# One edge tile in ten groups fetched row by row on the SyncE queue

## The chip, the cores and the metric

One core of one Trainium2 chip. Times are device microseconds (us) of that core; a run's time is its whole execution, and the time before is the median of three runs.

## The reference

One message-passing layer of a graph network, after a layer norm, with a residual. There are 12,500 nodes with 64 features and 412,500 edges with 32 features, sorted by their receiver. Cut to what matters:

```python
h = maximum(layernorm(x), 0)
msg_in = concat([h[senders], h[receivers], edge_features])      # 64 + 64 + 32
messages = silu(msg_in @ W1 + b1) @ W2 + b2                     # 64 wide
att = softmax(silu(msg_in @ Wa1 + ba1) @ Wa2 + ba2, axis=0)     # over all edges
aggregated = segment_sum(messages * att, receivers)
return x + silu(concat([h, aggregated]) @ Wu1 + bu1) @ Wu2 + bu2
```

## The kernel before

**First stage (to about 100 us).** For every node the sender's and the receiver's share of the first layer, both attention and message half, 128 numbers, are computed once and stored in the tables `ts_d` (senders) and `tr_d` (receivers) in device memory. A row of either is 512 bytes.

**The loop over groups.** Edges go in tiles of 128 and in groups of K = 8 tiles; there are NG = 403 groups. `one_pass` runs over them in a software pipeline written out by hand: at step g it calls `begin(g)`, then `load(g + 2)`, then `end(g)`, with pieces of the sums of earlier groups (`sum_up`) between.

- `load(g)` asks for everything of group g. On POOL, eight indirect DMAs (line 382), one per tile, each fetch 128 rows of `ts_d` by the edges' sender numbers, which lie in `src_sb`; they fill the eight planes of the tile `gs`, of which there are eight buffers. On SP, every four groups (NQ = 4), one DMA brings the edge features (`eo`, line 391), two bring the receivers' numbers (`db`, line 394), and one register load (line 369, called by `registers`) brings the first receiver of four groups at once. For each group two more SP DMAs (line 401) fetch a window of rows of `tr_d` into `wins`, at an address from such a register; there are three window buffers. DVE then makes a one-hot matrix in `eo` (line 405), and PE multiplies it, with the edge features below it, by the window (line 409), into the PSUM tile `pe`: the receiver's and the edge's share.
- `begin(g)` adds the gathered sender's share: DVE `gs = pe + gs` (line 414), then ACT takes the tanh (line 415).
- `end(g)` forms messages and attention logits on DVE. Every fourth group a running maximum is taken; later steps weigh the messages and sum them by receiver through PE (lines 477 to 508).

**Work beside the loop.** Between groups 16 and about 116, `node_bias` and `node_rest` (lines 276 to 305) prepare the update of the nodes; their loads and stores go through SP as well (lines 285, 294, 303, 305).

**Last stage (from about 4108 us).** The update of all nodes.

**Order.** Compute instructions of the loop stand in the order in which the program is written (`pin`). DMAs and register loads are not pinned: a scheduler puts them into their engine's stream by program order and by what it takes to be ready. [...]

Of the kernel before, what the change touches and what calls it, by code (L numbers as in the profile page):

```python
# [42 lines left out]
F32 = mybir.dt.float32  # L43
I32 = mybir.dt.int32
AF = mybir.ActivationFunctionType
ALU = mybir.AluOpType
AX = mybir.AxisListType
ENG = mybir.EngineType
# [3 lines left out]
P = 128  # L52
# [3 lines left out]
C = 2 * U  # L56
S1 = U + 1
K = 8
# [7 lines left out]
B = 4  # L66
NQ = 4
TABLES = 4
EPS = 1e-5
NEG = -3.0e38  # L70
BIG = 3.0e38
# [5 lines left out]
WHY = "a receiver's number; windows past the last node are padded"  # L77


@with_exitstack  # L80
def gnn_kernel(ctx: ExitStack, tc: tile.TileContext, n_edges, x, src, dst, dst_row, first, edge,
               weights, out):
    nc = tc.nc
    NB = x.shape[0] // P
    T = src.shape[1]
    NG = T // K
    NP = NB * P
# [6 lines left out]
    ts_d = dram.tile([NP, C], F32, name="ts_d")  # L94
# [12 lines left out]
    part, at = {}, 0  # L107
# [45 lines left out]
    with tc.tile_pool(name="node1", bufs=1) as node1, \  # L153
# [20 lines left out]
        pin = tc.keep_in_program_order  # L174
# [15 lines left out]
        eps = node1.tile([P, 1], F32, name="eps")  # L190
        nc.vector.memset(eps, EPS)
        xms, sqs, rstds, hs = {}, {}, {}, {}
# [60 lines left out]
        for c, nn in chunks:  # L253
            tr = node.tile([P, CB, C], F32, name="tr")[:, :nn, :]
            for b in range(0, nn, 4):
                n = min(4, nn - b)
                pn = node_ps.tile([P, 4, C], F32, name="pn", bufs=4)
                for i in range(0, n, 2):
# [8 lines left out]
        windows()  # L267

    one_pass(tc, n_edges, locals())
    again = nc.values_load(wrong[0:1, 0:1], min_val=0, max_val=1,  # L270
                           skip_runtime_bounds_check_because="it is the outcome of a comparison")
# [36 lines left out]
def one_pass(tc, n_edges, v):  # L308
    nc = tc.nc
    NB, T, NG, NP, CB = (v[k] for k in ("NB", "T", "NG", "NP", "CB"))  # L310
# [3 lines left out]
    ts_d, tr_d, bq_d, edge, dst_row = (v[k] for k in ("ts_d", "tr_d", "bq_d", "edge", "dst_row"))  # L314
# [8 lines left out]
    pin = tc.keep_in_program_order  # L323

    with ExitStack() as ctx:
# [16 lines left out]
        for w in wins:  # L342
            nc.vector.memset(w, 0.0)
            for r in range(2):
                rows = slice(WR + r * DE, WR + (r + 1) * DE)
                nc.vector.tensor_copy(w[rows, :, r, :], we[rows, None, :].to_broadcast([DE, 2, C]))
        with tc.tile_pool(name="work2", bufs=2) as work2, \
                tc.tile_pool(name="small", bufs=3) as small, \
                tc.tile_pool(name="pre_ps", bufs=AHEAD + 1, space=PSUM) as pre_ps, \
                tc.tile_pool(name="one_ps", bufs=1, space=PSUM) as one_ps:  # L350
            pes, gss, lgs, ps_, psums, sps, pps, ees, mts = ({} for _ in range(9))


            w2t_ps = one_ps.tile([P, 4, P], F32, name="mt")[:U, 0, :S1]
# [4 lines left out]
            nc.tensor.matmul(w2u_ps, w2t, wu1a, start=True, stop=True)  # L359
            nc.vector.tensor_copy(w2u, w2u_ps)  # L360
            at_sp, at_dve = {}, {}


            tr_w = bass.AP(tensor=tr_d.tensor, offset=tr_d.offset,
# [2 lines left out]
            def registers(g, engine, at):  # L367
                n = min(NQ, NG - g)
                _, regs = nc.values_load_multi_w_load_instructions(
                    base_sb[0:1, g:g + n], engines=[engine], min_val=0, max_val=NP - 1,  # L370
                    skip_runtime_bounds_check_because=WHY)
                for i in range(n):
                    at[g + i] = regs[i]

            def load(g):

                t = g * K
                if g % NQ == 0:
                    registers(g, ENG.SP, at_sp)
                gs = gss[g] = gather.tile([P, K, C], F32, name="gs")  # L380
                for j in range(K):
                    nc.gpsimd.indirect_dma_start(  # L382
                        out=gs[:, j, :], out_offset=None, in_=ts_d[:, :],
                        in_offset=bass.IndirectOffsetOnAxis(ap=src_sb[:, t + j:t + j + 1], axis=0))
                if g % NQ == 0:
                    n = min(NQ, NG - g) * E2
                    eo = work2.tile([P, NQ, E2], F32, name="eo")
                    db = work2.tile([WR, NQ, E2], I32, name="db")
                    for i in range(g, min(g + NQ, NG)):
                        ees[i] = eo[:, i - g, :], db[:, i - g, :]  # L390
                    nc.sync.dma_start(eo.rearrange("p g e -> p (g e)")[WR:, :n],
                                      edge[:, g * E2:g * E2 + n])
                    for r in range(2):
                        nc.sync.dma_start(
                            db.rearrange("p g e -> p (g e)")[r * R:(r + 1) * R, :n],
                            bass.AP(tensor=dst_row.tensor, offset=dst_row[r:r + 1, g * E2:].offset,
                                    ap=[[0, R], [1, n]]))
                eo, db = ees.pop(g)
                win = wins[g % WINS]
                for r in range(2):  # L400
                    nc.sync.dma_start(win[r * R:(r + 1) * R, :, r, :],
                                      tr_w[bass.ds(at_sp[g], R), :, :])
                for h in range(2):
                    e = slice(h * E2 // 2, (h + 1) * E2 // 2)
                    pin(nc.vector.tensor_scalar(eo[:WR, e], db[:, e], bj[:, g, h:h + 1], None,  # L405
                                                op0=ALU.is_equal))
                pe = pes[g] = pre_ps.tile([P, K, C], F32, name="pe")
                for q in range(H):
                    pin(nc.tensor.matmul(pe[:, 2 * q:2 * q + 2, :], eo[:, q * P:(q + 1) * P],  # L409
                                         win[:, q // 2, :, :], start=True, stop=True))  # L410

            def begin(g):

                pin(nc.vector.tensor_tensor(gss[g], pes[g], gss[g], ALU.add))  # L414
                pin(nc.scalar.activation(pes[g], gss[g], AF.Tanh))  # L415

            def end(g):
# [94 lines left out]
            at, weighed = [None, None], [0]  # L512
# [28 lines left out]
            for g in range(AHEAD):  # L541
                load(g)
            done = 0
            for g in range(NG):
# [3 lines left out]
                if more and g == NG - 1:  # L548
                    next(more)
                begin(g)  # L550
                if more and g < NG - 1:
                    next(more)
# [6 lines left out]
                if g + AHEAD < NG:  # L559
                    load(g + AHEAD)  # L560
# [36 lines left out]
        with tc.tile_pool(name="upd1", bufs=1) as upd1, \  # L597
# [14 lines left out]
            for c in range(0, NB, 2 * H):  # L612
                n = min(H, (NB - c) // 2)
# [32 lines left out]
def general(tc, n_edges, v, dst):  # L646
# [7 lines left out]
    with ExitStack() as ctx:  # L654
        keep = ctx.enter_context(tc.tile_pool(name="keep_g", bufs=1))
        act_d = dram.tile([P, T, S1], F32, name="act_d")
        sum_d = [dram.tile([NP + P, S1], F32, name=f"sum_d{r}") for r in range(TABLES)]
        before = keep.tile([P, P], F32, name="before")
# [15 lines left out]
        rows = (NP + P) // P  # L674
        for r in range(TABLES):
            flat = sum_d[r].rearrange("(p b) f -> p (b f)", p=P)
# [63 lines left out]
        with tc.tile_pool(name="sums_g", bufs=2) as work, \  # L740
                tc.tile_pool(name="sums_g_ps", bufs=2, space=PSUM) as sums_ps:
            for g in range(0, T, G):
# [3 lines left out]
                for k in range(0, ng, K):  # L746
# [26 lines left out]
                    for j in range(K):  # L773
                        nc.gpsimd.indirect_dma_start(
                            out=sum_d[(t + j) % TABLES][:, :],
                            out_offset=bass.IndirectOffsetOnAxis(ap=to[:, j:j + 1], axis=0),
# [6 lines left out]
        with tc.tile_pool(name="upd_g", bufs=2) as work, \  # L783
                tc.tile_pool(name="upd_g_ps", bufs=2, space=PSUM) as upd_ps:
            for c in range(0, NB, CB):
                part = work.tile([P, TABLES, CB, S1], F32, name="part")
                for r in range(TABLES):
                    nc.sync.dma_start(part[:, r], sum_v[r][:, c:c + CB, :])
                for r in range(1, TABLES):
                    nc.vector.tensor_tensor(part[:, 0], part[:, 0], part[:, r], ALU.add)  # L790
# [95 lines left out]
```

## Time and profile before

| | |
|---|---|
| median of three runs | 4173.35 us (4166.1 to 4174.21) |
| profiled execution: its own time | 4166.68 us |
| its span, first to last instruction | 4164.9 us |
| busy: POOL, DVE, PE, ACT | 73%, 69%, 54%, 14% |
| mean share of the 16 DMA engines | about 35% |
| granted TensorE clock | 0.635 |

The page lists groups of instructions by line, with busy time, mean duration and the idle time of the engine just ahead of them. SP runs no computation; what it does is issue DMAs and load registers, so it has no busy time on the page, and its queue is read from the views by source line and from its own waits ("SPq"). The shares are averages over three stages. The loop, from about 105 to 4100 us, is 96% of the span.

### The profile page before, as it was taken

The numbers are of one execution on the slowest core, as the hardware profiler recorded it, in microseconds if no ns is written. First come the engines' busy times: TensorE is split into PE (matmuls) and PEld (weight loads), VectorE is DVE, ScalarE is ACT, GpSimd is POOL, SyncE is SP. The second block draws the span as 40 slices with busy tenths as digits, with TensorE's granted clock in tenths as the row PEclk, the third lists the DMA queues.
The fourth block names the chain that finished last, engine by engine and source line by source line (L and its number), as shares of the span: only waits on it lengthen the run. The fifth ranks groups of instructions, "written<-read, shape, count | busy, mean of one in ns | idle before, by whom it ended". The sixth has DMA issues, their size and how long they took to land.

```text
span 4164.9 us, 43769 instructions
## 1 busy us (share of the span) xinstructions
PE 2237.8 (54%) x10980; PEld 1678.3 (40%) x10980; DVE 2873.2 (69%) x7698; ACT 600.9 (14%) x1230; POOL 3052.8 (73%) x3236
## 2 busy tenths in 40 slices
PE   5544555545545555555555455555555555555555
PEld 4433434333434343443444334343344443444444
DVE  5867767766677676666766667666676666666668
ACT  2211111111111111111111111111111111111112
POOL 3777777777777777777777777777777777777772
PEclk8666666666666666666656655666565666656665
DMA  7433433333333333333333332333323333333323
GB/s 269 103 92 95 102 100 96 101 95 101 101 89 90 89 81 90 82 88 90 80 90 83 87 89 80 90 82 87 90 80 89 83 88 90 80 90 85 85 77 111
DMA packets 230871, 392.46 MB, mean 94 GB/s; under 512 B 97745, under 2 KB 156370, under 8 KB 217426
## 3 DMA queue, kind: packets, MB, share of 16 engines
q0 software_dynamic: 103168, 211.49, 19.1%
q1 hardware_dynamic: 125778, 167.76, 15.2%
q10 hardware_dynamic: 1664, 10.32, 0.6%
q8 instruction: 91, 1.49, 0.1%
q14 instruction: 170, 1.39, 0.1%
HBM read 363.56 MB, written 25.72 MB: 93 GB/s over the span
## 4 chain that ended last, share of the span: by engine, by line


## 5 line engine op out<-in xcount | busy, mean ns | idle before, releaser
L382 POOL DMA_INDIRECT gs<-ts_d,src_sb x3224 | 3051.2, 946 | 1038.3 <-issue 930.2
L409 PE MATMUL pe<-wins,eo 128*128 128x256 f32 x3224 | 1395.8, 608 | 1178.2 <-issue 1122.1
L409 PEld LDWEIGHTS pe<-wins,eo 128*128 128x128 f32 x3224 | 953.6, 310 | 1453.1 <-issue 1189.0
L414 DVE TENSOR_TENSOR gs<-pe,gs 128x1024 f32<-128x1024 f32 x403 | 491.8, 1220 | 1116.6 <-DMA gs<-ts_d,src_sb 1103.8
L415 ACT ACTIVATE pe<-gs 128x1024 f32<-128x1024 f32 x403 | 415.7, 1031 | 2760.5 <-DVE gs L414 2267.5
L477 DVE TENSOR_SCALAR wt<-iota_w,dloc,p 128x40 f32<-128x40 f32 x3224 | 725.2, 316 | 0.1
L483 PE MATMUL sp<-wt,acts 128*65 128x40 f32 x6448 | 586.0, 261 | 0.9 <-DVE wt L477 0.9
L483 PEld LDWEIGHTS sp<-wt,acts 128*65 128x65 f32 x6448 | 535.3, 173 | 26.7 <-DVE wt L477 1.0
L453 PE MATMUL mt<-ident,mx 128*128 128x128 f32 x103 | 48.6, 472 | 530.3 <-DVE sums L507 526.9
L425 DVE SCALAR_TENSOR_TENSOR acts<-pe,gs 128x512 f32<-128x512 f32 x403 | 271.9, 675 | 27.7 <-ACT pe L415 27.6
L433 DVE TENSOR_TENSOR pe<-pe,w_all 128x512 f32<-128x512 f32 x403 | 281.4, 698 | 12.8
L431 DVE SCALAR_TENSOR_TENSOR pe<-pe,gs 128x512 f32<-128x512 f32 x403 | 280.4, 696 | 11.2
L436 DVE TENSOR_REDUCE lg<-pe 128x8 f32<-128x512 f32 x403 | 276.9, 687 | 10.3
L405 DVE TENSOR_SCALAR eo<-db,bj 64x256 f32<-64x256 int32 x806 | 270.3, 373 | 8.0 <-DMA db<-in_dst_row_dram 0.4
L494 PEld LDWEIGHTS mt<-ss,w2u 65*64 65x64 f32 x806 | 99.2, 175 | 392.6 <-issue 378.6
L453 PEld LDWEIGHTS mt<-ident,mx 128*128 128x128 f32 x103 | 18.8, 182 | 543.1 <-DVE sums L507 538.9
L494 PE MATMUL mt<-ss,w2u 65*64 65x40 f32 x806 | 149.9, 280 | 160.5 <-DVE gm L460 148.0
L464 ACT ACTIVATE scale<-fall 128x1 f32<-128x1 f32 x103 | 20.9, 203 | 510.2 <-DVE fall L463 510.2
L508 DVE COPY sums<-nmax 64x40 f32 x403 | 79.1, 196 | 9.0 <-issue 0.2
L489 ACT COPY ss<-sp 65x40 f32<-65x40 f32 x403 | 73.5, 182 | 28.6 <-PE sp L483 28.6
L507 DVE TENSOR_TENSOR sums<-sums,mt 64x40 f32 x300 | 53.6, 179 | 3.5 <-PE mt L494 2.4
L290 ACT COPY bu<-mt 64x512 f32<-64x512 f32 x24 | 25.9, 1078 | 149.1 <-PE mt L287 149.1
(89 smaller groups left out, 591.3 us busy)
## 6 DMA issues: line engine op xcount, KB each, us to landing
gs<-ts_d,src_sb POOLq DMA_INDIRECT x3224
eo<-in_edge_dram SPq DMA_DIRECT2D x100, 512.0 KB
db<-in_dst_row_dram SPq DMA_DIRECT2D x200, 256.0 KB
wins<-tr_d SPq DMA_DIRECT2D x806, 32.0 KB
ts_d<-ts SPq DMA_DIRECT2D x5, 896.0 KB
tr_d<-tr ACTq DMA_DIRECT2D x5, 896.0 KB
hT_d<-hT ACTq DMA_DIRECT2D x1, 3136.0 KB
hb<-in_x_dram SPq DMA_DIRECT2D x24, 128.0 KB
```

What stands on the lines that cost most here:

```text
L382: nc.gpsimd.indirect_dma_start(out=gs[:, j, :], out_offset=None, in_=ts_d[:, :], in_offset=bass.IndirectOffsetOnAxis(ap=src_sb[:, t + j:t ...
L405: pin(nc.vector.tensor_scalar(eo[:WR, e], db[:, e], bj[:, g, h:h + 1], None, op0=ALU.is_equal))
L409: pin(nc.tensor.matmul(pe[:, 2 * q:2 * q + 2, :], eo[:, q * P:(q + 1) * P], win[:, q // 2, :, :], start=True, stop=True))
L414: pin(nc.vector.tensor_tensor(gss[g], pes[g], gss[g], ALU.add))
L415: pin(nc.scalar.activation(pes[g], gss[g], AF.Tanh))
L425: pin(nc.vector.scalar_tensor_tensor(acts[g % ACTS][:, :, 0:U], th[:, :, U:C], 1.0, gs[:, :, U:C], op0=ALU.add, op1=ALU.mult))
L431: pin(nc.vector.scalar_tensor_tensor(att, th[:, :, 0:U], 1.0, gs[:, :, 0:U], op0=ALU.add, op1=ALU.mult))
L433: pin(nc.vector.tensor_tensor(att, att, wa2[:, None, :].to_broadcast([P, K, U]), ALU.mult))
L436: pin(nc.vector.tensor_reduce(lgs[s][:, k:k + K], att, AX.X, ALU.add))
L477: pin(nc.vector.tensor_scalar(wt[:, j, :], iota_w[:, j // H, :], dloc[:, g * K + j:g * K + j + 1], p[:, k + j:k + j + 1], op0=ALU.is_equal ...
L483: pin(nc.tensor.matmul(sp, acts[g % ACTS][:, j, :], wt[:, j, :], start=j == 0, stop=j == K - 1))
L494: pin(nc.tensor.matmul(pp, w2u, sps.pop(g), start=True, stop=True))
```

## The change

In 39 of the 403 groups (g = 10, 20, ... 390) the last of the eight tiles is no longer gathered by POOL. Its 128 rows are fetched by 128 DMAs from SP, one row and one partition each, into a tile of its own, `one_gs`.

- The sender numbers of the tile come as one row of a new input, `src_row`, which holds the same numbers as `src` in their order; `rows_ahead` asks for them five groups before the first row is fetched.
- `rows(g)`, called in `load(g)` just after the windows, fetches ROWS = 13 rows (11 in the last of ten groups) of the tile that is due ten groups later. Register loads bring the row numbers, LOADS = 4 at a time: four loads in a group of 13 rows, for 4, 4, 4 and 1 numbers.
- `begin(g)` adds seven planes of `gs` in one instruction and the eighth, from `one_gs`, in another.

The last tile asked for is that of group 390, as 400 is not below NG - 4 = 399.

```diff
--- before.py
+++ after.py
@@ -66,6 +66,9 @@
 B = 4
 NQ = 4
 TABLES = 4
+EVERY = 10
+ROWS = 13
+LOADS = 4
 EPS = 1e-5
 NEG = -3.0e38
 BIG = 3.0e38
@@ -78,7 +81,7 @@
 
 
 @with_exitstack
-def gnn_kernel(ctx: ExitStack, tc: tile.TileContext, n_edges, x, src, dst, dst_row, first, edge,
+def gnn_kernel(ctx: ExitStack, tc: tile.TileContext, n_edges, x, src, src_row, dst, dst_row, first, edge,
                weights, out):
     nc = tc.nc
     NB = x.shape[0] // P
@@ -348,7 +351,7 @@
                 tc.tile_pool(name="small", bufs=3) as small, \
                 tc.tile_pool(name="pre_ps", bufs=AHEAD + 1, space=PSUM) as pre_ps, \
                 tc.tile_pool(name="one_ps", bufs=1, space=PSUM) as one_ps:
-            pes, gss, lgs, ps_, psums, sps, pps, ees, mts = ({} for _ in range(9))
+            pes, gss, lgs, ps_, psums, sps, pps, ees, mts, alone = ({} for _ in range(10))
 
 
             w2t_ps = one_ps.tile([P, 4, P], F32, name="mt")[:U, 0, :S1]
@@ -360,6 +363,35 @@
             nc.vector.tensor_copy(w2u, w2u_ps)
             at_sp, at_dve = {}, {}
 
+            rows_at, rows_to = {}, {}
+
+            def rows_ahead(g):
+                if g < NG - 4:
+                    t = g * K + K - 1
+                    rows_at[g] = small.tile([1, P], I32, name="one_src", bufs=2)
+                    nc.sync.dma_start(rows_at[g], v["src_row"][:, t * P:(t + 1) * P])
+
+            def rows(g):
+                if g == 0:
+                    rows_ahead(EVERY)
+                if g % EVERY == 0:
+                    rows_at.pop(g, None)
+                    rows_to.clear()
+                    if g + EVERY in rows_at:
+                        rows_to[g + EVERY] = one = work2.tile([P, C], F32, name="one_gs")
+                        alone[g + EVERY] = one
+                if g % EVERY == EVERY // 2:
+                    rows_ahead(g + EVERY // 2 + EVERY)
+                for at, to in rows_to.items():
+                    i = g % EVERY * ROWS
+                    for a in range(i, min(i + ROWS, P), LOADS):
+                        n = min(LOADS, P - a)
+                        _, regs = nc.values_load_multi_w_load_instructions(
+                            rows_at[at][0:1, a:a + n], engines=[ENG.SP], min_val=0, max_val=NP - 1,
+                            skip_runtime_bounds_check_because=WHY)
+                        for k in range(n):
+                            nc.sync.dma_start(to[a + k:a + k + 1, :], ts_d[bass.ds(regs[k], 1), :])
+
 
             tr_w = bass.AP(tensor=tr_d.tensor, offset=tr_d.offset,
                            ap=[[C, NP + WR - SHIFT], [SHIFT * C, 2], [1, C]])
@@ -378,7 +410,7 @@
                 if g % NQ == 0:
                     registers(g, ENG.SP, at_sp)
                 gs = gss[g] = gather.tile([P, K, C], F32, name="gs")
-                for j in range(K):
+                for j in range(K - (g in alone)):
                     nc.gpsimd.indirect_dma_start(
                         out=gs[:, j, :], out_offset=None, in_=ts_d[:, :],
                         in_offset=bass.IndirectOffsetOnAxis(ap=src_sb[:, t + j:t + j + 1], axis=0))
@@ -400,6 +432,7 @@
                 for r in range(2):
                     nc.sync.dma_start(win[r * R:(r + 1) * R, :, r, :],
                                       tr_w[bass.ds(at_sp[g], R), :, :])
+                rows(g)
                 for h in range(2):
                     e = slice(h * E2 // 2, (h + 1) * E2 // 2)
                     pin(nc.vector.tensor_scalar(eo[:WR, e], db[:, e], bj[:, g, h:h + 1], None,
@@ -411,7 +444,10 @@
 
             def begin(g):
 
-                pin(nc.vector.tensor_tensor(gss[g], pes[g], gss[g], ALU.add))
+                n = K - (g in alone)
+                pin(nc.vector.tensor_tensor(gss[g][:, :n, :], pes[g][:, :n, :], gss[g][:, :n, :], ALU.add))
+                if n < K:
+                    pin(nc.vector.tensor_tensor(gss[g][:, n, :], pes[g][:, n, :], alone.pop(g), ALU.add))
                 pin(nc.scalar.activation(pes[g], gss[g], AF.Tanh))
 
             def end(g):
@@ -863,6 +899,7 @@
     arrays = {
         "x": padded(x, nb * P),
         "src": np.ascontiguousarray(padded(src, t * P).reshape(t, P).T),
+        "src_row": padded(src, t * P)[None],
         "dst": np.ascontiguousarray(dst_row.reshape(t, P).T),
 
         "dst_row": np.ascontiguousarray(dst_row.reshape(t // 2, 2, P).transpose(1, 0, 2).reshape(2, -1)),
```

## The prediction

> **What bounds the kernel now.** The page's busy table comes first, then its costliest groups. The page's chain that ended last is empty for this run, so the bound has to be read from groups and waits.
>
> ```profile
> PE 2237.8 (54%) x10980; PEld 1678.3 (40%) x10980; DVE 2873.2 (69%) x7698; ACT 600.9 (14%) x1230; POOL 3052.8 (73%) x3236
> L382 POOL DMA_INDIRECT gs<-ts_d,src_sb x3224 | 3051.2, 946 | 1038.3 <-issue 930.2
> ```
>
> POOL is at 73%, DVE at 69%; neither looks full. But POOL's idle time in front of the gathers is 930 us of "issue": it waits for nobody, it needs that time itself. The timeline of POOL shows the beat:
>
> ```profile
> 2011.29 0.94 POOL L382 DMA_INDIRECT gs<-ts_d,src_sb  x1 [0.30 <-issue]
> 2012.54 0.94 POOL L382 DMA_INDIRECT gs<-ts_d,src_sb  x1 [0.30 <-issue]
> 2013.79 0.94 POOL L382 DMA_INDIRECT gs<-ts_d,src_sb  x1 [0.30 <-issue]
> ```
>
> 0.94 busy and 0.30 between: one gather each 1.25 us, eight a group, 10.0 us a group. The first starts at 56.4 and the last at 4091.0 (the view of line L382), so (4091.0 - 56.4) / 3223 = 1.252 us is the beat of the whole loop, start to end. POOL bounds the kernel. The waits, longest first, agree: DVE's longest own wait is for what POOL fetched, and POOL's wait for others is small.
>
> ```profile
> DVE gs L414 <- DMA gs<-ts_d,src_sb: 1103.8, 274, 14.6
> ...
> POOL gs L382 <- DMA gs<-ts_d,src_sb: 60.8, 193, 1.7
> ```
>
> **SP, where the new work goes.** Its queue is in the waits of SP and in the views by source line (min/median/max ns):
>
> ```profile
> SPq L401 <- PE pe L409: 1877.9, 264, 22.2
> ...
> SPq L305 <- DVE hb L304: 117.2, 25, 7.8
> SPq L616 <- PE mt L494: 57.0, 1, 57.0
> SPq L303 <- PE mt L287: 45.9, 23, 3.3
> ...
> SPq L285 <- DMA xb_d<-hb: 37.2, 24, 1.9
> ```
>
> ```profile
> L401 SPq DMA_DIRECT2D wins<-tr_d x806: 316/317/938, 92.1 to 4050.8; - x162
> ```
>
> ```profile
> L369 SPq TENSOR_LOAD <-base_sb x101: 294/299/1443, 86.0 to 4022.7; - x101
> ```
>
> ```profile
> L166 SPq DMA_DIRECT2D base_sb<-in_first_dram x1: 307/307/307, 7.0 to 7.0; - x1
> ```
>
> SP is ahead: it mostly waits for PE to give back one of three windows (L401). The lines L303, L305 and L285 are the node work, which lies between 109 and 1168 us only (first and last start); their waits are for results just asked for, so they are not all slack.
>
> **What the Trainium skill says.** "DMA: Bandwidth & Descriptors", section "Issuing engines are not separate DMA queues": issuing from another engine saves only sequencer time. Here that time is just what binds (1.25 us of POOL a gather), so moving a gather can pay. Same page, "Why a DMA increments its semaphore by 16 and not by 1": a DMA from SP whose slowest dimension gives one engine is put on that one, and the sequencer itself writes the rest of the semaphore. The one single-partition DMA of this trace, base_sb, took SP 0.307 us, no more than the others. Same page, "Latency and other measured facts": about 600 ns for a register load; this trace has 0.299 us for four registers, and I use that.
>
> **The change, part by part.** Groups 10, 20, ... 390 qualify (400 is past NG - 4 = 399): 39 tiles.
>
> Removed: 39 gathers, 39 x 1.252 = **48.8 us** of POOL. Ten groups then take it 79 x 1.252 = 98.9 us, not 100.2.
>
> Added on SP per tile: 128 row DMAs, 9 x 4 + 3 = 39 loads, one ask for row numbers. A window DMA with a register in its address: a pair spans 0.82 to 0.84 us in the timeline and one is 0.317, so the next starts 0.51 later; 0.19 of it is address arithmetic and turn-round. With 0.307 for one partition: 0.50 a row. From below 0.44 (arithmetic partly shared), from above 0.62 (a separate wait in front, or an issue as slow as hT_d's 0.606). 128 x 0.50 = 64.0. Loads: 0.30 and 0.05 to the next, 39 x 0.35 = 13.7; from above, at the skill's 0.6, 25, as most of these loads do not start at a multiple of four numbers. The ask: 0.4. Sum **78.1 us per ten groups**.
>
> SP's present work, without waits, per four groups: 8 x 0.51 windows, eo 0.53, db 0.43 + 0.63, load 0.35, six waits' handling 0.3: 6.3, so 15.7 per ten groups. Node work adds per four groups 0.45 + 0.44 + 2 x 0.65 + 0.54 + 0.2 = 2.9, so 7.4 per ten.
>
> So SP needs 93.8 of POOL's 98.9 us in the late stage, but **101.2 of 98.9 in the node stage** (groups 16 to 116), before any wait. SP is in order; the trace shows eight completion semaphores in turn on its queue, each DMA waiting for the one eight before. A row lands, I estimate, like a window (median 1.7 us in the records) and eight rows take 4; only eo (5.1 us to land) makes SP wait, an estimated 0.6 per four groups, 1.5 per ten. The node work's waits (117.2 + 45.9 + 37.2 + 16.6 for L294) / 25 = 8.7 us per four groups; rows stand in them now, and I keep a third, 2.9, which is 7.2 per ten: from below 0, from above all, 22. Node stage: 101.2 + 1.5 + 7.2 = 109.9.
>
> What is queued behind: the windows, which PE needs (L409), then DVE's L414. How much lateness is free? Windows can start at 92.1; PE at about 94 + 9.5 g if SP paces, the gathers land at 68 + 9.9 g (56.4, one group's 9.9, some 2 to land). So at group 16 the loop is 20 us behind POOL, where now it has caught up (DVE takes 6.4 us a group at 126 to 145 us). POOL stops when gather g + 8 finds none of the eight buffers free: at 56.4 + 79 + 9.9 g, so 135 + 9.9 g; with some 10 us from the matmul to the end of a group, lateness of 55 us is free. Node stage: 10 x (109.9 - 98.9) = 110 more, 130 in all, 75 beyond the cover. Net 75 - 48.8 = **26 us slower**. Later SP has about 3.5 us to spare per ten groups and regains the rest before the end; the last 13 groups have no rows.
>
> DVE: L414 split in two, one more instruction and up to eight semaphore waits, some 0.2 + 0.4 us in 39 groups, 23 us in all, covered by DVE's 31% idle time; if DVE were the bound, they would count. The rows' bytes replace the gather's, so DMA load (33%) stays.
>
> The profiled execution took 4166.7 us (span 4164.9, 1.8 around it): 4193. The median of the runs, 4173.35, lies 6.7 above it: **4199**.
>
> **Rivals.**
> 1. SP keeps up. For: 93.8 in the late stage, and the node waits may vanish as rows fill them. Then up to 102.4 us per ten groups in the node stage are free, and the whole 48.8 comes: 4125. The point of no change is 107.3. Chance of a visible gain 0.28.
> 2. The forecast, SP late in the node stage alone: 4182 to 4260. With it, near no change: 0.09; slower 0.40.
> 3. SP bounds the whole loop, for instance with 0.56 to a row because each needs a wait of its own (0.055): 103 late (4.1 over, 28 times), 117.6 in the node stage: 115 + 187 + 20 - 55 - 49 = 218 slower: 4391. The point is 98.9 / 128: a row price of 0.53. Chance 0.19.
> 4. The rows run in bursts: DMAs without a fixed place can be ordered ahead (db goes out before older windows at 2006 to 2010 us). 128 rows in front of a window are 78 us, against three windows and 55 us of cover; some 25 us a tile, 39 times: 5100. Chance 0.04.
> That the gathers are not dropped (3224 stays) would leave 4173 plus SP's work; the code shows no reason.
>
> **How the numbers follow.** A measurement of this kernel can tell about 0.2% (8 us). Faster 0.28 (rival 1), within 0.09, slower 0.40 + 0.19 + 0.04 = 0.63. Predicted is the likeliest case, 4199; its own range is 4182 to 4260. The range for 8 in 10 reaches from rival 1 (4122) into rival 3 (4350): 0.12 lie above, a little below.
>
> **What would show it.** Gathers 3185; row DMAs 4992 at about 0.31 us on SP; SP's wait for PE at L401, 1878 us, down below 400; in the node stage POOL with gaps over 0.3 us, waiting for DVE, and PE waiting for wins; after 1200 us POOL at its 1.25 beat. Wrong if POOL never waits (rival 1), or if PE's waits for wins run to the end (rival 3).

## The result and the profile after

The changed kernel takes 5286.07 us (median of 4 runs, 5277.05 to 5286.85) against 4173.66 us before: ratio 1.266, interval 1.265 to 1.268. That is 1112 us slower; the forecast was 26 us slower, with a range that ended at 4350.

The page after, its busy line and its costliest groups:

```profile
PE 2333.5 (44%) x10980; PEld 1741.0 (33%) x10980; DVE 2884.4 (55%) x7737; ACT 615.0 (12%) x1230; POOL 3015.5 (57%) x3197
...
L414 POOL DMA_INDIRECT gs<-ts_d,src_sb x3185 | 3014.0, 946 | 2171.0 <-issue 2090.1
L442 PE MATMUL pe<-wins,eo 128*128 128x256 f32 x3224 | 1484.6, 640 | 2734.0 <-DMA wins<-tr_d 1131.3
...
L438 DVE TENSOR_SCALAR eo<-db,bj 64x256 f32<-64x256 int32 x806 | 252.2, 351 | 1213.1 <-DMA db<-in_dst_row_dram 1106.8
```

The 39 gathers are gone (3185) and each of the others costs what it did (946 ns). But POOL's idle time has grown from 1038 to 2171 us, PE waits 1131 us for windows and DVE 1107 us for receivers' numbers. Both come through SP. That POOL's "issue" is now a wait shows in the view of the gathers' line, where an EVENT_SEMAPHORE is POOL's queue waiting for a free buffer; the first line is before, the second after:

```profile
L382 POOLq EVENT_SEMAPHORE  x399: 17/43/43, 52.9 to 4074.7; - x200
```

```profile
L414 POOLq EVENT_SEMAPHORE  x399: 17/3492/20662, 52.9 to 5169.9; - x200
```

Before, such an instruction takes 43 ns, so the buffer is free; after, the median is 3.5 us and the longest 20.7. POOL has become a follower. SP's own waits, where before the wait for PE at the windows' line stood at 1877.9 us, now read:

```profile
SPq L393 <- DMA db<-in_dst_row_dram: 56.7, 109, 1.2
...
SPq L433 <- PE pe L442: 20.8, 4, 7.4
```

SP no longer waits for PE: it is the bound. What fills it is in the views of its new lines (min/median/max ns):

```profile
L393 SPq DMA_DIRECT2D one_gs<-ts_d x6045: 224/228/292, 95.8 to 5107.8; - x195
L393 SPq EVENT_SEMAPHORE  x682: 17/17/17, 107.1 to 5102.2; - x171
```

```profile
L389 SPq TENSOR_LOAD <-one_src x1521: 301/1117/1731, 95.2 to 5105.9; - x191
```

Two things here are not as forecast. The row DMAs are 6045, not 4992: 155 a tile instead of the 128 that the description of the change has too. And a register load takes 1.117 us in the median, not 0.30. Issuing a row is cheaper than assumed, 0.228 us instead of 0.307.

**Why 155.** The loop over a group runs from i to i + 13 in steps of four, and `n = min(LOADS, P - a)` looks only at the end of the tile. The load at i + 12 so brings four numbers and fetches rows i + 12 to i + 15, and the next group fetches the last three again: 9 x 16 + 11 = 155. The description's loads of "4, 4, 4 and 1 numbers" are 4, 4, 4 and 4. A second fetch of a row has to wait for the first, with an EVENT_SEMAPHORE in front: the view has 682, and the kernel with sixteen rows a group below, which fetches no row twice, has none on that line. They cost little, some 0.08 us each in the records.

**Why 1.1 us.** A group's numbers begin at a multiple of 13. The view of the load line in two windows of time, first in a group that begins at row 52, then in the next, at row 65:

```profile
L389 SPq TENSOR_LOAD <-one_src x4: 310/554/597, 2534.6 to 2542.6; - x4
```

```profile
L389 SPq TENSOR_LOAD <-one_src x5: 1062/1124/1145, 2546.4 to 2559.1; - x5
```

Over all tiles the records give one pattern (medians): where the first number is a multiple of four (16 bytes) the load takes 0.55 us behind a row and 0.31 or 0.48 behind a window's DMA; elsewhere it takes 1.12 behind a row and 0.87 or 1.06 behind a window's DMA. The lower of each pair stands in every fourth group, where SP has loaded the windows' registers just before. The last load of a tile, of three numbers off a multiple, takes 0.93. Behind DMAs of the node work loads take longer still, up to 1.73. Three groups of ten (rows 0, 52, 104) begin on a multiple of four.

**The order of SP's stream.** The timeline of SP after shows the windows each between sixteen rows, as the program has them, and in the whole trace no more than 16 rows stand between two groups' windows, so nothing ran ahead in bursts:

```profile
2505.81 0.86 SPq L433 DMA_DIRECT2D wins<-tr_d  x2
2508.04 10.54 SPq L393 DMA_DIRECT2D one_gs<-ts_d  x16
2518.83 0.86 SPq L433 DMA_DIRECT2D wins<-tr_d  x2
2521.05 10.20 SPq L393 DMA_DIRECT2D one_gs<-ts_d  x16
2531.35 0.48 SPq L423 DMA_DIRECT2D eo<-in_edge_dram  x1
2531.89 1.04 SPq L426 DMA_DIRECT2D db<-in_dst_row_dram  x2
2533.73 0.87 SPq L433 DMA_DIRECT2D wins<-tr_d  x2
2535.14 9.73 SPq L393 DMA_DIRECT2D one_gs<-ts_d  x16
2545.12 0.86 SPq L433 DMA_DIRECT2D wins<-tr_d  x2
```

From one pair of windows to the next it is 11 to 15 us here. Counted over the starts of the windows in the whole trace, ten groups take 125 us from group 120 on and 139 in the node stage (groups 16 to 116), against 100 and 101 before.

### The profile page after: what moved, and what is told of

Read it like the earlier page. It is cut to its first block, busy times and chain, and to the rows that moved or that the text cites. A ratio compares the mean times of both kernels' runs of the same rounds, so it can differ in the third digit from the quotient of the medians.

```text
span 5284.1 us, 64333 instructions
## 1 busy us (share of the span) xinstructions
PE 2333.5 (44%) x10980; PEld 1741.0 (33%) x10980; DVE 2884.4 (55%) x7737; ACT 615.0 (12%) x1230; POOL 3015.5 (57%) x3197
## 4 chain that ended last, share of the span: by engine, by line
## 5 line engine op out<-in xcount | busy, mean ns | idle before, releaser
L414 POOL DMA_INDIRECT gs<-ts_d,src_sb x3185 | 3014.0, 946 | 2171.0 <-issue 2090.1
L442 PE MATMUL pe<-wins,eo 128*128 128x256 f32 x3224 | 1484.6, 640 | 2734.0 <-DMA wins<-tr_d 1131.3
L442 PEld LDWEIGHTS pe<-wins,eo 128*128 128x128 f32 x3224 | 1009.9, 328 | 3040.8 <-issue 2820.4
L438 DVE TENSOR_SCALAR eo<-db,bj 64x256 f32<-64x256 int32 x806 | 252.2, 351 | 1213.1 <-DMA db<-in_dst_row_dram 1106.8
L513 DVE TENSOR_SCALAR wt<-iota_w,dloc,p 128x40 f32<-128x40 f32 x3224 | 737.0, 314 | 0.1
L448 DVE TENSOR_TENSOR gs<-pe,gs 128x1024 f32<-128x1024 f32 (+1 forms) x403 | 486.2, 1206 | 56.5 <-issue 27.9
L290 PE MATMUL mt<-hb,w_all 65*64 65x512 f32 (+1 forms) x50 | 47.3, 1050 | 80.7 <-DMA hb<-hT_d 80.7
```

The source lines that it names most:

```text
L414: nc.gpsimd.indirect_dma_start(out=gs[:, j, :], out_offset=None, in_=ts_d[:, :], in_offset=bass.IndirectOffsetOnAxis(ap=src_sb[:, t + j:t ...
L448: pin(nc.vector.tensor_tensor(gss[g][:, :n, :], pes[g][:, :n, :], gss[g][:, :n, :], ALU.add))
L513: pin(nc.vector.tensor_scalar(wt[:, j, :], iota_w[:, j // H, :], dloc[:, g * K + j:g * K + j + 1], p[:, k + j:k + j + 1], op0=ALU.is_equal ...
```

## The experiments

Two of the kernels below ran on a chip where the kernel before takes 4165.95 us. All others, and these two another time, ran on chips where it takes 5470 to 5490 us. In the traces from those chips about one in ten of SP's small instructions (moves, register arithmetic, semaphore waits) takes over 0.2 us, most of these some 0.7, up to 1.4; the medians on DVE, ACT and POOL are as elsewhere. That this is what makes the kernel before slow there is not shown, as it has no trace from such a chip. Sizes are read from the chip with 4166; the others are used for order and direction only. Line L433 of the kernel with POOL alone changed shows such a chip, against a longest MOVE of 122 ns before:

```profile
L433 SPq MOVE wins<-tr_d x806: 3/29/1411, 154.0 to 5335.1; - x162
```

**All loads at a multiple of four.**

```diff
-                    i = g % EVERY * ROWS
+                    i = g % EVERY * ROWS // LOADS * LOADS
```

> One thing changed: each group's first row number is rounded down to a multiple of four, so that all 39 register loads of a tile start at a multiple of four numbers (16 bytes); 39 loads stay, the rows are 156 a tile instead of 155. Theory A (the loads' addresses): loads off a multiple of four took 1.06 to 1.13 us, the others 0.31 behind a window and 0.55 behind a row; all loads now 0.31 to 0.60, some 20 us per ten groups instead of 37 to 45. SP per ten groups: 156 x 0.41 + 39 x 0.54 + 15.7 + 0.4 = 101, just over POOL's 98.9: 4180 to 4280 us. Theory B (the row DMAs themselves hold SP's queue and the loads wait behind them, whatever their address): loads stay near 1.1 us and the time at 5250 to 5320 us.

> The kernel of e1_aligned again (all 39 loads at a multiple of four numbers, 156 rows), on another chip. Theory A: SP 101 us per ten groups against POOL's 98.9: 4180 to 4280 us. Theory B: 5250 us and over.

Measured where before takes 4166: 4759.9 us, ratio 1.143 (1.141 to 1.145). The loads:

```profile
L389 SPq TENSOR_LOAD <-one_src x1521: 300/554/1140, 95.0 to 4577.4; - x191
```

The same number of loads takes 825 us in sum instead of 1429. Theory B falls: the loads were slow by their address, not by the rows in front of them. The edit also halves the EVENT_SEMAPHOREs in front of rows, from 682 to 342; at 0.08 us each that is 27 us of the 526 between 5286 and 4760. But the time I expected, 4180 to 4280, missed: ten groups take 111 us late, not 101, and 126 in the node stage. From one row to the next it is 0.46 us in the mean, not 0.41, as SP waits for landings, that is, for data of earlier DMAs to arrive (106 us in all for those of `db`).

**Sixteen rows a group, none twice, loads at a multiple of four.**

```diff
-ROWS = 13
+ROWS = 16
```

> ROWS = 16: eight groups of ten fetch 16 rows each, 128 rows a tile, none twice, 32 loads, all at a multiple of four numbers. Theory A: 128 x 0.41 + 32 x 0.54 + 15.7 + 0.4 = 86 us of SP per ten groups, 94 in the stage with node work, both under POOL's 98.9; POOL is the bound again with 39 gathers less: 4125 to 4140 us, faster than before by some 0.9 to 1.2%. Theory B: SP is still held by the row DMAs: over 4800 us.

> The kernel of e3_sixteen again (ROWS = 16: 128 rows a tile, 32 aligned loads), on another chip: the first took 5481 us for the kernel before instead of 4174, with stalls of 0.7 us in SP's stream that the kernel before does not show on the chip of its profile. Theory A: SP needs 86 us per ten groups, 94 in the stage with node work, under POOL's 98.9: 4125 to 4140 us. Theory B (the row DMAs hold SP's queue): over 4800 us, as on the first chip (1.21 times before).

Measured where before takes 4166: 4231.51 us, ratio 1.0163 (1.0149 to 1.0177). Theory B would have left it above 4800. The forecast of a gain missed: it is 1.6% slower. The page of this kernel shows where, in its 40 slices of POOL:

```profile
POOL 3777766666676777777777777777777777777772
```

The sixes are the node stage. The windows of time, here 300 to 700 and 2000 to 2400 us (busy us and count of each engine):

```profile
300.00:700.00 400.00, 192.07 (x928) 137.21 (x928) 252.51 (x670) 52.22 (x105) 283.86 (x300) 0.62 0.39 92
...
2000.00:2400.00 400.00, 215.18 (x1098) 162.84 (x1097) 283.43 (x774) 52.98 (x113) 302.50 (x320) 0.65 0.38 90
```

300 gathers in the first, 320 in the second; 320 is POOL's full beat, as before. POOL's gaps over 0.45 us in the trace add up to 110 us beyond the usual 0.30 of each, all of them before 1600. 110 less the 48.8 saved is 61; measured are 65.6. SP's pace is 111 us per ten groups in the node stage, some 95 from group 120 to 280, where SP makes up its lateness, and then POOL's 99. Expected were 94 and 86: rows cost 0.46 in the mean with their waits, and the node work's waits had been left out.

**No row twice, loads left as they are.**

```diff
-                        n = min(LOADS, P - a)
+                        n = min(LOADS, i + ROWS - a, P - a)
```

> One thing changed: the last load of a group stops at the thirteenth row, so that no row is fetched twice: 128 rows a tile instead of 155, still 39 loads, in nine groups of ten the last of one number. Theory A: 128 x 0.41 = 53 us of rows, loads of four off a multiple of four at 1.1 us each and of one number at about 0.5: 32 to 36 us; with 15.7 and 0.4, 102 to 105 us per ten groups against POOL's 98.9: 4280 to 4400 us. Theory B: the time goes by the row DMAs alone, 128 / 155 of SP's queue: 1110 us over before x 0.83, 5090 us.

> The kernel of e2_no_twice again (128 rows a tile, none fetched twice, loads still off a multiple of four), on a chip where before takes 4166 to 4174 us. Theory A with the prices of the runs so far, a row 0.42 and its waits 0.02, loads of four 1.1 in seven groups of ten: 128 x 0.44 + 36 + 17 + 1 = 110 us per ten groups against e1's 112 and the changed kernel's 127: 4600 to 4780 us. If the rows alone set the time, the same rows as e3: 4230 us.

All five runs were on chips where before takes 5470 to 5483: 7017 to 7071 us, ratios 1.280 to 1.293. The size on the other kind of chip was not measured. Its traces add one thing, the loads of a single number. A group that begins at row 26, first its three loads of four numbers, then its load of one:

```profile
L389 SPq TENSOR_LOAD <-one_src x3: 1052/1121/1127, 2192.8 to 2198.5; - x3
```

```profile
L389 SPq TENSOR_LOAD <-one_src x1: 529/529/529, 2201.3 to 2201.3; - x1
```

Behind a row, one number off a multiple of four takes 0.53 us, three took 0.93 and four 1.12: each further number adds 0.2 us. On a multiple, four numbers cost about what one does (0.55).

**The changed kernel there, unedited, and with the 39 gathers put back.**

> The changed kernel itself, unedited, for the chips where before takes 5480 us, on which it has no time yet: if SP bounds the loop there, it takes what e4 (the same with the gathers kept) takes, 7600 to 7680 us; if POOL's gathers count, 49 us less than e4. Where before takes 4166 to 4174: 5270 to 5300 us as on the first chip.

```diff
-                for j in range(K - (g in alone)):
+                for j in range(K):
```

> The changed kernel with the 39 gathers put back on POOL; SP does all its new work and DVE still adds the rows from their own tile. If SP bounds the loop (theory A or B), POOL's 48.8 us lie in its idle time: 5270 to 5300 us, the changed kernel's 5286. If POOL still counted: 5335 us.

The unedited kernel takes 7547.97 us there (1.376, 1.373 to 1.378). With the gathers it takes 7658.29 (1.398, 1.396 to 1.401), on another chip of the same kind. 110 us more is neither none nor 49: the difference of chips is not separated from the gathers, so this run decides nothing.

Set beside the unedited 7548, aligned loads give 7182 (-366), no row twice 7017 to 7071 (some -500), both together, sixteen a group, 6649 (-899). These too are different chips, and before differs between them by up to 19 us. Both effects are there, and about add up.

**POOL's part alone.** The gathers are left out, no rows are fetched, and the eighth plane adds a constant.

```diff
-                rows(g)
+                if g % EVERY == 0 and EVERY <= g + EVERY < NG - 4:
+                    alone[g + EVERY] = v["bias"]
```

> The other half alone: the 39 gathers are left out and nothing takes their place on SP; the eighth plane of those groups adds a constant tile of weights instead of the senders' rows, so this part of the computation is left out. DVE's split instruction stays. If POOL's beat of 1.252 us sets the time, 39 gathers less are 48.8 us: 4120 to 4128 us. If DVE's split or another engine takes the gain back: over 4135 us.

> The kernel of e5_pool_alone again, on a chip where before takes 4166 to 4174 us: 39 gathers less, no rows fetched, and a constant tile added in their place, which leaves out that part of the computation. POOL's beat: 48.8 us less, 4117 to 4125 us. If something else holds the loop at its pace: over 4135 us.

5442.02 and 5435.26 us where before takes 5481 and 5478: ratios 0.993 (0.991 to 0.994) and 0.992 (0.990 to 0.993), 39 and 42 us less. That is near the 48.8 forecast, but on those chips POOL is not the bound: its queue waits for buffers, 4.2 us in the median.

```profile
L414 POOLq EVENT_SEMAPHORE  x399: 17/4152/39154, 53.1 to 5294.5; - x200
```

So POOL's beat alone does not explain it, and why some 40 us go there stays open. That the beat gives 48.8 where before takes 4166 was not measured.

**Rows only behind the node stage.** Sixteen rows a group, 27 tiles; the loads are held in program order besides, a second difference from the kernel with sixteen rows above.

```diff
-                if g < NG - 4:
+                if 120 < g < NG - 4:
...
+                        for ld in lds:
+                            pin(ld)
```

> ROWS = 16 with aligned loads, and only for tiles whose rows are fetched after the stage with node work: groups 130, 140, ... 390, 27 tiles. The loads are also held in program order, which the build needs. If e3's loss was the node stage alone (SP over POOL there: POOL 283.9 of 400 us busy between 300 and 700 us, 302.5 after 2000), POOL keeps its beat throughout and 27 gathers less show: 27 x 1.25 = 34 us, 0.8% faster, 4128 to 4140 us where before is 4166 to 4174. If SP is over POOL in the late stage too (its waits counted), no gain or a loss: 4170 to 4300 us.

> The kernel of e8_late_only once more, for a chip where before takes 4166 to 4174 us: if e3's loss was the node stage alone, 4128 to 4140 us; if SP is over POOL in the late stage too, 4170 to 4300. Where before takes 5480 us: 6150 to 6240 again.

Five runs on chips where before takes 5470 to 5488: 6150 to 6235 us, ratios 1.125 to 1.138. There it is clearly slower than before: in the trace of the last of them ten groups take 127 us in the node stage, where no rows are fetched, and 160 from group 120 on; with POOL alone changed, on such a chip, they take 126 and 133. Whether it is faster where before takes 4166 stays open; the late stage of the kernel with sixteen rows, with POOL at 320 gathers in 400 us, is all that speaks for it. No version that computes the whole result has beaten the kernel before on any chip here.

## Why the prediction was wrong

The steps that failed are two terms of SP's sum per ten groups: the rows, of which 155 are fetched and not 128, and the register loads, 38.6 us and not 13.7. With them SP needs 125 us in the late stage where 95.3 were forecast, and that is over POOL's 98.9, not under it.

- **What bounds before, and the gain.** POOL, 1.25 us a gather, as the trace of before shows. In the change 39 gathers go, as counted. That they are worth 48.8 us was not measured by itself.
- **Rows a tile.** Wrong, and a misreading of the code: 128 in the step "128 row DMAs", 155 in fact. The last chunk of a group was taken to be one number because 13 = 4 + 4 + 4 + 1; no line of the program says so. With the addresses alone put right it is still 4760 us, above the range; with sixteen rows a group, none twice, it is 4231, inside it.
- **Price of a row.** The step "0.50 a row", measured 0.41 from start to start without waits (0.228 to issue), 0.45 in the mean with them. Too high.
- **Price of a load.** The step "39 x 0.35 = 13.7", measured 1429 us / 39 tiles = 36.6, and 0.05 after each: 38.6. The bound from above, 25, was too low as well. The prediction saw that the loads do not start at a multiple of four and took for its bound the 0.6 us of the Trainium skill ("DMA: Bandwidth & Descriptors", section "Latency and other measured facts"); measured are 0.30 to 1.73 here, so that is neither a floor nor a price. The only loads in the trace of before, 0.299 us, all start at a multiple of four, so they could not price the others.
- **The sum.** Late stage, forecast 93.8 with 1.5 for waits. Measured prices: 155 x 0.41 = 63.6, loads 38.6, present work 15.7, the ask 0.3, second fetches' waits 17 x 0.08 = 1.4, other waits some 4 (gaps in SP's stream): 124. The trace has 125. Over POOL's 98.9 from end to end, so the lateness is never made up.
- **Which case.** Rival 3's mechanism came true, SP bounding the loop from end to end, with loads and twice-fetched rows in place of the extra wait on every row that it named. It had 0.19, and its time, 4391, was far too low. Its limit of 0.53 a row is 0.50 and the spare 3.6 us over 128 rows; the "98.9 / 128" that stands there is not that sum. Rival 4's time, 5100, lay near by chance: its bursts are not in the timeline.
- **The node stage.** The forecast's own mechanism, SP late there and in time again behind it, is real, as the kernel with sixteen rows shows: forecast 95.3 and 109.9 us of SP per ten groups, measured some 95 and 111. That it agrees so well is luck: its 128 rows cost 58.8 us with their waits where 64.0 were forecast, its 32 loads 18.9 where 13.7 were forecast for 39. The cover of 55 us was too large: POOL lost 110 us there, not 75. The program that I thought I read, 128 rows and 39 loads of 4, 4, 4 and 1, is the one with no row twice, whose time where before takes 4166 was not measured; with its dear loads it was expected at 4600 to 4780.

Where the 1112 us went, in this order of edits: 526 with the loads' addresses (5286 to 4760), 528 with the 28 twice-fetched rows and seven loads more (4760 to 4231), 66 with the node stage net of the gain; the sum is 8 over, the difference of before between the two chips. Between rows and the seven loads the 528 is not split by a run. By the prices it is 28 x 0.42 = 11.8 us and 7 x 0.6 = 4.2, together 16.0; from one kernel to the other ten groups take 16.5 us less of SP in the late stage.

DVE's split cost little, as forecast: 1.08 + 0.28 us instead of 1.22, 39 times.

## What to carry to other kernels

Work moved off the bounding engine must fit the beat of the engine it is moved to, counted as instructions that the program really issues: run the innermost loop by hand for one full turn, with its last chunk. A price read from a trace holds for the operands that the trace had; ask what in address, count or neighbour differs for the new instruction. Before an engine becomes the bound its waits look like spare time: SP's 1878 us in front of the windows here. Count every instruction in its stream, stage by stage.

## What the runs showed of the hardware

- A register load of four numbers on SP: with the first at a multiple of 16 bytes 0.31 or 0.48 us behind a window's DMA and 0.55 behind a single-row DMA; at other addresses 0.87 to 1.12. Off a multiple, behind a row, the price goes by the count, 0.53, 0.93 and 1.12 us for one, three and four numbers. Why a load takes longer behind a row was not tried.
- SP issues a DMA of one 512-byte row to one partition in 0.228 us, 0.41 from start to start with a register in its address; a window of 64 such rows takes 0.317 and 0.51. So 64 times the rows cost SP 0.09 us more.
- On five chips one in ten of SP's small instructions took over 0.2 us, up to 1.4, in the traces; the kernel before takes 5480 us there instead of 4170, and the changed kernel 7548 instead of 5286. What makes SP slow there is not known.
